# A state-space layer's token sums: four column groups by halves of tokens, and a new order of steps

## The chip, the cores and the metric

The kernel runs on one core of a Trainium2 chip. The metric is device time in microseconds for one execution. The inputs and outputs are float32, and the kernel computes in float32 throughout.

## The reference, cut to what matters

Two layers on 8 batches of 512 tokens with 256 channels. Layer 0 adds an attention (16 heads) and a mixture of 16 experts to the input. Layer 1 adds a state-space block and a linear layer on values rounded to a six-bit grid. The change concerns layer 1 and the weights that it uses:

```python
xz = einsum('bld,ed->ble', xn, in_proj_w); x, z = split(xz, 2)       # 512 channels each
u = silu(conv4(x) + conv1d_b)                                         # causal, four taps, per channel
x_dbl = einsum('bld,rd->blr', u, x_proj_w)                            # 16 dt_low, 16 B, 16 C
delta = softplus(einsum('blr,dr->bld', dt_low, dt_proj_w) + dt_proj_b)
h_t = exp(delta_t * A) * h_(t-1) + delta_t * B_t * u_t                # 512 channels x 16 states
y_t = sum over the 16 states of h_t * C_t  +  u_t * D_param
out = (y * silu(z)) @ out_proj_w.T  +  dequantized(xn) @ dequantized(weight).T + bias
x = x + out
```

## The kernel before, in words

**Layer 0.** `norm_and_route` loads all tokens, normalizes them, chooses experts and scatters the rows to `xs` in DRAM. Then a loop over 32 head groups runs with the experts' matmuls between them. Its order is the program's order on each engine. Before `norm_and_route` the kernel calls `layer1_weights`, which loads all weights of layer 1 through ACT's DMA queue (w_in, w_x, w_dt, w_out, prm, bias, a) and last `wq`, the 256 x 256 weight that is quantized on DVE and POOL (`quantize`) and transposed on PE to `wdT`. The tiles of `wq` and its temporaries lie on the side of SBUF where `xn`, the loaded tokens, comes next.

**Layer 1** has 8 batches. For each there are 16 steps `j`; step `j` treats 32 channels at all 512 tokens. The 128 rows of a step's tiles are four groups of 32 channels, and each group holds four of the 16 states in its free dimension (`SK` = 4, 4 x 512 columns). A step has these parts:

- `decay` (ACT, L715): four exponentials make `da` from the step sizes `step`, which `load_steps` fetches from DRAM for two steps at a time, four times over (one for each group of rows).
- `spread` (PE, L722): a matmul with `sel` copies the 32 rows of `du` (delta times u) onto 128 rows of PSUM.
- `scan` (L728 and L730 on DVE, L734 on POOL): `dbu` = spread times `B`, a scan over 2048 columns gives `h`, and POOL multiplies `h` by `C`. There are four `h` tiles.
- `sums` (PE, L742 and L747), for two steps at once: sums over states. A skip matmul with a diagonal of D_param starts the PSUM tile of a block of 128 channels (every fourth step), then eight matmuls of 512 columns add the two steps' `h` on two groups of 32 columns.
- `gated` (DVE, L751): for a block of 128 channels, y times silu(z).

The loop `for g in range(B * NB)` writes the order by hand: scan(g), then decay and spread of g + 1, then what is due now (`later`: sums two steps after, gated three steps after, and the previous batch's `result` and `put`, four of each, in steps 3 to 7), `load_steps` at even steps, and then one piece of `prepare` for the next batch. `prepare` is a generator of 16 pieces: load x and gather expert rows (two pieces), scale and add and store x (L583 to L585), statistics (L590 to L598), normalize and transpose (L602 to L615), in_proj for x (two pieces, L622 and L626), convolution (two pieces, L635), in_proj for z (two pieces), x_dbl, absolute value to logarithm of the step sizes (L668 to L676), a correction (L678, L680), delta and its store (L685, L686), du and the load of B (L690). The six pieces of `quantize` (L494 to L497; L500; L502 to L506; L509, L510; L512, L513; L515, L516) are called among them. C is loaded after a batch's last step into the one tile that it has. Every engine executes its instructions in this order, and SP issues the loads and stores in this order too.

PSUM holds four banks for `dbu`, one for `spread`, one for `sum` and two (`bank`) for all else. `result` multiplies, for 128 tokens, the quantized rows by `wdT`, the bias by ones, and four blocks of z by `w_out`; ACT copies it to `o`, and `put` adds x on POOL and stores.

A float32 matmul of the program is two matmul instructions in the trace.

Of the kernel before, what the change touches and what calls it, by code (L numbers as in the profile page):

```python
# [34 lines left out]
XR = DTR + 1 + 2 * DS  # L35
# [44 lines left out]
class Kernel:  # L80
# [437 lines left out]
    def layer1_weights(self, w_in, w_x, w_dt, w_out, prm, w_q, bias):  # L518
        nc, one = self.nc, self.weights
        self.w_in = one.tile([P, KC, 2 * DI], F32, name="w_in")  # L520
        nc.scalar.dma_start(out=self.w_in, in_=w_in.rearrange("(kc p) e -> p kc e", p=P))

        self.w_x = one.tile([P, NC, XR], F32, name="w_x")
        nc.gpsimd.memset(self.w_x[:, :, DTR : DTR + 1], 0.0)
        w_x = w_x.rearrange("(c p) r -> p c r", p=P)
        nc.scalar.dma_start(out=self.w_x[:, :, 0:DTR], in_=w_x[:, :, 0:DTR])
        nc.scalar.dma_start(out=self.w_x[:, :, DTR + 1 :], in_=w_x[:, :, DTR:])
        self.w_dt = one.tile([33, DI], F32, name="w_dt")
        nc.scalar.dma_start(out=self.w_dt[0:DTR, :], in_=w_dt)
        nc.scalar.dma_start(out=self.w_dt[DTR : DTR + 1, :], in_=prm[:, DT_B].rearrange("d one -> one d"))  # L530
        self.w_out = one.tile([P, NC, C], F32, name="w_out")
        nc.scalar.dma_start(out=self.w_out, in_=w_out.rearrange("(c p) e -> p c e", p=P))
        self.prm = one.tile([P, NC, 7 + DS], F32, name="prm")
        nc.scalar.dma_start(out=self.prm, in_=prm.rearrange("(c p) k -> p c k", p=P))
        self.bias = self.w_dt[32:33, 0:C]
        nc.scalar.dma_start(out=self.bias, in_=bias)

        self.a = one.tile([P, NB, SK], F32, name="a")
        for q in range(SQ):
            nc.scalar.dma_start(  # L540
                out=self.a[ts(q, 32), :, :],
                in_=prm[:, 7 + SK * q : 7 + SK * (q + 1)].rearrange("(j p) k -> p j k", p=32),
            )
        nc.scalar.activation(self.a, self.a, AF.Exp)
        nc.vector.tensor_single_scalar(self.a, self.a, -1.0, ALU.mult)
# [13 lines left out]

    def in_proj(self, xnT, col):  # L560
        ps = self.bank()
        for kc in range(KC):
            self.nc.tensor.matmul(ps, lhsT=self.w_in[:, kc, ts(col, P)], rhs=xnT[:, kc, :], start=kc == 0, stop=kc == KC - 1)  # L563
        return ps

    def prepare(self, b):
# [17 lines left out]
        nc.gpsimd.tensor_tensor(x, x, y, ALU.add)  # L584
        nc.sync.dma_start(out=rows, in_=x)  # L585
        yield
# [53 lines left out]
        for c in (0, 1):  # L640
            nc.scalar.copy(z[:, c, :], self.in_proj(xnT, NC + c))
        yield
        next(quant, None)
        for c in (2, 3):
            nc.scalar.copy(z[:, c, :], self.in_proj(xnT, NC + c))
# [9 lines left out]
        nc.scalar.activation(x_dbl, ps[:XR, :], AF.Identity, bias=self.ident[:XR, DTR : DTR + 1])  # L655
        me["bc"] = self.dram.tile([2 * DS, N], F32, name="bc")
        nc.sync.dma_start(out=me["bc"], in_=x_dbl[DTR + 1 :, :])
        yield


        def steps_of(c):
            ps = self.bank()
            nc.tensor.matmul(ps, lhsT=self.w_dt[: DTR + 1, ts(c, P)], rhs=x_dbl[: DTR + 1, :], start=True, stop=True)  # L663
            return ps

        s = one.tile([P, NC, N + 3], F32, tag="rows", name="s")[:, :, 3:]
        for c in range(NC):
            nc.scalar.activation(s[:, c, :], steps_of(c), AF.Abs)  # L668
# [5 lines left out]
        me["du"] = [self.six.tile([P, N], F32, name="delta") for _ in range(NC)]  # L674
# [8 lines left out]
        for c in range(NC):  # L683
            delta = me["du"][c]
            nc.vector.scalar_tensor_tensor(delta, steps_of(c), 0.0, delta, ALU.max, ALU.add)  # L685
            nc.sync.dma_start(out=me["steps"][ts(c, P), :], in_=delta)  # L686
# [8 lines left out]
    def load_steps(self, b, c):  # L695

        t = self.three.tile([P, 2, N], F32, name="step")
        rows = self.batch[b]["steps"][ts(c, 64), :].rearrange("(r d) t -> d r t", d=32)
        for q in range(SQ):
            self.nc.sync.dma_start(out=t[ts(q, 32), :, :], in_=rows)  # L700
        self.batch[b]["step", c] = t
# [17 lines left out]
    def spread(self, b, j):  # L719
        c, r = divmod(j, 4)  # L720
        ps = self.spread_pool.tile([P, N], F32, name="spread")
        self.nc.tensor.matmul(ps, lhsT=self.sel[ts(r, 32), :], rhs=self.batch[b]["du"][c][ts(r, 32), :], start=True, stop=True)  # L722
# [13 lines left out]
    def sums(self, b, j):  # L736

        nc, me = self.nc, self.batch[b]
        c, r = divmod(j, 4)
        if r == 0:  # L740
            y = me["sum", c] = self.sum_pool.tile([P, N], F32, name="sum")
            nc.tensor.matmul(y, lhsT=self.skip[:, c, :], rhs=me["u"][:, c, :], start=True, stop=False)  # L742
        y = me["sum", c]
        pair = [(j + i, me.pop(("h", j + i))) for i in range(2)]
        for k in range(SK):
            for i, h in pair:
                nc.tensor.matmul(y[ts(i % 4, 32), :], lhsT=self.sel[:, 0:32], rhs=h[:, k, :], start=False, stop=k == SK - 1)  # L747
# [19 lines left out]
    def result(self, b, j):  # L767
        nc, me = self.nc, self.batch[b]
        ps = self.bank()[:, :C]
        for kc in range(KC):  # L770
            nc.tensor.matmul(ps, lhsT=me["xdT"][:, kc, ts(j, P)], rhs=self.wdT[:, kc, :], start=kc == 0, stop=False)
        nc.tensor.matmul(ps, lhsT=self.ones[32:33, :], rhs=self.bias, start=False, stop=False)
# [132 lines left out]
```

## Time and profile before

| | |
|---|---|
| median of three runs | 2473.65 us (2471.86 to 2474.25) |
| profiled execution | 2472.3 us, span 2470.2 us |
| granted PE clock, mean | 0.87 |
| layer 0, last matmul | ends at 1119.8 us |
| layer 1, first scan | starts at 1216.95 us |
| last of the 128 scans | starts at 2434.95 us |
| one batch, first scan to first scan | 149.6 (batch 0), 156.9 to 157.1 (batches 1 to 6) |

Starts of the 16 scans of a batch, one to the next, batch 3, from step 0: 7.3, 12.0, 7.3, 13.6, 7.1, 13.6, 9.7, 15.2, 7.8, 9.9, 7.3, 9.2, 11.9, 7.8, 7.3, 9.9 us.

How to read it: the page gives busy time of each engine (PE matmuls, PEld weight loads, DVE, ACT, POOL), forty slices of the span with the busy share in tenths, and groups of instructions. A line of the waits says which engine and line waited for which, the total in us, how often, and the longest. A line of the windows gives a stretch, its length, the busy us of each engine with the number of instructions, the granted PE clock and the DMA engines' share. A line of the timeline gives start, duration, engine, line, instruction, out<-in, shapes, count and, in brackets, the idle time before it and what ended it. "128*32 128x512" is a weight tile of 128 rows and 32 columns and an operand of 128 rows and 512 columns.

### The profile page before, as it was taken

Reading aid. Unit: us, or ns where it says so; the run is one execution under the profiler, and the core shown is the slowest. Engines: PE = TensorE matmul, PEld = TensorE weight load, DVE = VectorE, ACT = ScalarE, POOL = GpSimd, SP = SyncE. Lnnn points to the kernel's source line nnn. Section 1 sums busy time; section 2 is a strip of 40 time slices with the busy share of each in tenths; the row PEclk is TensorE's granted clock in tenths of the full one; section 3 lists DMA queues with packets and bytes.
Section 4 is the critical chain, followed back from the end, with each engine's and each line's share of the span. In section 5 each row is a group of like instructions: output and inputs, shape, how many; then the busy total and the mean of one; then the engine's idle time right before and its main releaser. Section 6 shows DMA issues by size and latency. Waiting matters only on the chain.

```text
span 2470.2 us, 21235 instructions
## 1 busy us (share of the span) xinstructions
PE 2022.4 (82%) x8040; PEld 836.1 (34%) x8040; DVE 1546.1 (63%) x1240; ACT 921.0 (37%) x1364; POOL 1006.4 (41%) x513
## 2 busy tenths in 40 slices
PE   2747999999999999995496796987968869688666
PEld 2513444444444444442131231422314224132222
DVE  3423554555555555531498878888788787887784
ACT  0002333333333333432445353353543635436231
POOL 4231010100000000005466668676776767767554
PEclk9958999999999999997687797887968879688778
DMA  6012111121211111101402213032131221402220
GB/s 204 13 49 94 47 61 50 62 81 53 77 46 62 45 62 46 62 6 40 113 17 77 62 51 102 24 88 51 56 90 41 82 57 36 111 31 74 50 60 9
DMA packets 104808, 150.81 MB, mean 61 GB/s; under 512 B 13937, under 2 KB 75122, under 8 KB 102658
## 3 DMA queue, kind: packets, MB, share of 16 engines
q1 hardware_dynamic: 90896, 132.97, 18.3%
q0 software_dynamic: 3072, 8.39, 1.2%
q10 hardware_dynamic: 10738, 8.10, 1.1%
q8 instruction: 63, 1.03, 0.2%
q14 instruction: 39, 0.32, 0.0%
HBM read 113.24 MB, written 36.18 MB: 60 GB/s over the span
## 4 chain that ended last, share of the span: by engine, by line
PE 54%; DVE 19%; POOL 12%; DMA 6%; issue 5%; ACT 4%; SPq 1%; ACTq 0%; DVEq 0%; POOLq 0%
PE s L287 11%; DVE h L730 8%; PE bank L389 7%; POOL h L734 7%; PE bank L379 5%; PE sum L747 5%; PE av L318 5%; DVE dbu L728 4%; PE bank L274 3%; PE bank L563 2%; DMA xs<-xn,to_i 2%; PE spread L722 2%; PE bank L635 2%; PE bank L248 2%; PE bank L663 2%
## 5 line engine op out<-in xcount | busy, mean ns | idle before, releaser
L734 POOL TENSOR_TENSOR h<-h,C 128x2048 f32<-128x2048 f32 x128 | 599.0, 4680 | 372.4 <-DVE h L730 333.2
L730 DVE TENSOR_TENSOR_SCAN h<-da,dbu 128x2048 f32<-128x2048 f32 x128 | 565.8, 4420 | 109.2 <-PE sum L747 77.9
L309 DVE TENSOR_REDUCE qk<-t 128x2 f32<-128x1024 f32 x256 | 313.7, 1225 | 387.5 <-PE t L287 387.5
L305 ACT ACTIVATE e<-s 128x1024 f32<-128x1024 f32 x256 | 262.0, 1024 | 437.5 <-PE t L287 408.3
L715 ACT ACTIVATE da<-step,a 128x511 f32<-128x511 f32 x512 | 325.2, 709 | 251.3 <-DVE h L730 185.3
L722 PE MATMUL spread<-delta,c_sb 32*128 32x512 f32 x256 | 191.3, 835 | 216.2 <-DVE dbu L728 215.8
L728 DVE TENSOR_TENSOR dbu<-spread,B 128x2048 f32<-128x2048 f32 x128 | 293.4, 2292 | 66.9 <-PE spread L722 52.1
L287 PE MATMUL t<-kT,qT 32*128 32x512 f32 x1024 | 298.0, 659 | 8.1 <-DVE qk L309 8.1
L287 PE MATMUL s<-qmT,kT 32*128 32x512 f32 x1024 | 290.4, 643 | 17.1 <-DVE qmT L99 15.6
L747 PE MATMUL sum<-h,c_sb 128*32 128x512 f32 x1024 | 293.1, 725 | 4.9 <-POOL h L734 4.9
L347 POOL TENSOR_TENSOR x<-x,o 128x256 f32<-128x256 f32 x32 | 23.2, 725 | 531.5 <-DVE o L345 531.5
L389 PE MATMUL bank<-w_sb,hT 128*128 128x256 f32 (+1 forms) x768 | 183.6, 382 | 0.0
L261 POOL TENSOR_TENSOR qk<-cos_t,sin_t 128x512 f32<-128x512 f32 x32 | 40.7, 1271 | 316.6 <-DVE sin_t L257 316.4
L379 PE MATMUL bank<-xeT,w_sb 128*128 128x320 f32 x512 | 161.7, 438 | 0.0
L722 PEld LDWEIGHTS spread<-delta,c_sb 32*128 32x128 f32 x256 | 47.9, 231 | 328.7 <-DVE dbu L728 201.2
L747 PEld LDWEIGHTS sum<-h,c_sb 128*32 128x32 f32 x1024 | 63.6, 130 | 249.7 <-issue 238.4
L389 PEld LDWEIGHTS bank<-w_sb,hT 128*128 128x128 f32 (+1 forms) x768 | 126.5, 174 | 43.4 <-issue 16.2
L318 PE MATMUL av<-e,v 128*32 128x512 f32 x1024 | 136.9, 607 | 0.0
L663 PE MATMUL bank<-x_dbl,w_dt 17*128 17x512 f32 x128 | 88.7, 829 | 41.0 <-DVE delta L685 28.1
L563 PE MATMUL bank<-xnT,w_in 128*128 128x512 f32 x256 | 118.1, 606 | 0.0
L287 PEld LDWEIGHTS s<-qmT,kT 32*128 32x128 f32 x1024 | 77.9, 184 | 114.2 <-issue 75.2
L635 PE MATMUL bank<-xs,taps 128*128 128x512 f32 x256 | 113.8, 597 | 1.6 <-ACT xdT L760 1.6
(172 smaller groups left out, 2246.8 us busy)
## 6 DMA issues: line engine op xcount, KB each, us to landing
w_sb<-in_w_dram SPq DMA_DIRECT2D x32, 1024.0 KB, 7.6
step<-steps SPq DMA_DIRECT2D x256, 128.0 KB, 3.1
mid<-x SPq DMA_DIRECT2D x16, 512.0 KB, 3.1
steps<-delta SPq DMA_DIRECT2D x32, 256.0 KB, 2.0
B<-bc SPq DMA_DIRECT2D x32, 256.0 KB, 4.9
C<-bc SPq DMA_DIRECT2D x32, 256.0 KB, 4.9
xs<-zero ACTq DMA_DIRECT2D x1, 5120.0 KB, 27.6
xn<-in_x_dram SPq DMA_DIRECT2D x8, 512.0 KB, 13.3
```

The costliest lines, as they stand in the source:

```text
L287: self.nc.tensor.matmul(ps, lhsT=lhsT[rows, :], rhs=rhs[rows, :], start=True, stop=True)
L305: nc.scalar.activation(e, s, AF.Exp, scale=D**-0.5)
L309: nc.vector.tensor_reduce(self.qk[b % 2][:, m, ds(NG * g + 2 * (1 - pair), 2), D], t, AX.X, ALU.max, negate=True)
L318: self.nc.tensor.matmul(self.av[G][ts(a, 2 * D), :], lhsT=self.v[b % 2][:, m, NG * g + a, :], rhs=self.e[G, m, a // 2][:, a % 2, :], start ...
L379: nc.tensor.matmul(ps[:, :CAP], lhsT=w1_sb[:, kc, ts(f, P)], rhs=xeT[:, kc, :], start=kc == 0, stop=kc == KC - 1)
L389: nc.tensor.matmul(ps[:r, :C], lhsT=hT[:, f, ds(j * P, r)], rhs=w2_sb[:, f, :], start=f == 0, stop=f == NF - 1)
L715: self.nc.scalar.activation(da[:, k, 1:], self.batch[b]["step", c][:, r, 1:], AF.Exp, scale=self.a[:, j, k : k + 1])
L722: self.nc.tensor.matmul(ps, lhsT=self.sel[ts(r, 32), :], rhs=self.batch[b]["du"][c][ts(r, 32), :], start=True, stop=True)
L728: nc.vector.tensor_tensor(dbu, bcast(me.pop(("spread", j))[:, None, :], [P, SK, N]), me["B"], ALU.mult)
L730: nc.vector.tensor_tensor_scan(h.rearrange("p k t -> p (k t)"), self.da[j % len(self.da)].rearrange("p k t -> p (k t)"), dbu.rearrange("p ...
L734: nc.gpsimd.tensor_tensor(h, h, me["C"], ALU.mult)
L747: nc.tensor.matmul(y[ts(i % 4, 32), :], lhsT=self.sel[:, 0:32], rhs=h[:, k, :], start=False, stop=k == SK - 1)
```

## The change

- `sums`: the tile of a block now holds tokens 0 to 255 on rows 0 to 63 and tokens 256 to 511 on rows 64 to 127; the columns are 256 tokens for the block's first 64 channels and 256 for its second. A pair of steps fills four groups of 32 rows with matmuls of 256 columns. The skip matmul becomes four of 64 weight columns and 256 columns.
- z is computed in that layout (`in_proj_z`), and `result` takes it so: for two token blocks at once, on 64 rows each, in both `bank` tiles.
- `spread` takes all 128 rows of a `du` tile with a weight tile (`quarter`) that is zero outside the 32 rows wanted.
- x_proj's output has 96 rows (XR) instead of 49, with dt_low twice, on rows 32 and 64, so that `steps_of` makes two blocks at once on two groups of rows, in both banks.
- The weights of layer 1 other than `wdT` are loaded at the start of layer 1, after the first piece of `prepare(0)`; `w_out` is loaded twice (for two halves of rows), w_dt and dt_low's part of w_x too. Taps and skip are made after three more pieces.
- Buffers: two tiles of step sizes instead of three, five of delta instead of six.
- Order: `result` in steps 3 and 5; its additions one step later and its stores two steps later; `load_steps` ahead of what is due; `quantized_transposed` in step 5; the pieces of `prepare` at steps 12, 13, 14 of the batch before and 0, 1, 2, 4, 6 to 14, with the store of x moved to the next piece.

The diff (cut):

```diff
@@ layer1_weights, now called by layer1 through other_weights
+        self.w_x = one.tile([P, NC, XR], F32, name="w_x")
+        nc.gpsimd.memset(self.w_x, 0.0)
+        for at in (1, 2):
+            nc.scalar.dma_start(out=self.w_x[:, :, ds(32 * at, DTR)], in_=w_x[:, :, 0:DTR])
+        nc.scalar.dma_start(out=self.w_x[:, :, 0:32], in_=w_x[:, :, DTR:])
+        self.w_dt = one.tile([XR, DI], F32, name="w_dt")
+        nc.gpsimd.memset(self.w_dt, 0.0)
+        for at in (32, 64):
+            nc.scalar.dma_start(out=self.w_dt[at : at + DTR, :], in_=w_dt)
+            nc.scalar.dma_start(out=self.w_dt[at + DTR : at + DTR + 1, :], in_=prm[:, DT_B].rearrange("d one -> one d"))
+        for t in range(2):
+            nc.scalar.dma_start(out=self.w_out[ts(t, 64)], in_=w_out.rearrange("(c h p) e -> p c h e", h=2, p=64))
...
+    def in_proj_z(self, xnT, c):
+        ps = self.bank()
+        for h in range(2):
+            for kc in range(KC):
+                for t in range(2):
+                    self.nc.tensor.matmul(
+                        ps[ts(t, 64), ts(h, N // 2)], lhsT=self.w_in[:, kc, ds(DI + c * P + h * 64, 64)],
+                        rhs=xnT[:, kc, ts(t, N // 2)], start=kc == 0, stop=kc == KC - 1,
+                    )
+        return ps
@@ prepare
         nc.gpsimd.tensor_tensor(x, x, y, ALU.add)
+        yield
         nc.sync.dma_start(out=rows, in_=x)
-        yield
...
         def steps_of(c):
-            ps = self.bank()
-            nc.tensor.matmul(ps, lhsT=self.w_dt[: DTR + 1, ts(c, P)], rhs=x_dbl[: DTR + 1, :], start=True, stop=True)
-            return ps
+            both = [self.bank() for _ in range(2)]
+            for i, ps in enumerate(both):
+                rows = ts(1 + i, 32)
+                nc.tensor.matmul(ps, lhsT=self.w_dt[rows, ts(c + i, P)], rhs=x_dbl[rows, :], start=True, stop=True)
+            return both
@@ spread
-        self.nc.tensor.matmul(ps, lhsT=self.sel[ts(r, 32), :], rhs=self.batch[b]["du"][c][ts(r, 32), :], start=True, stop=True)
+        self.nc.tensor.matmul(ps, lhsT=self.quarter[:, r, :], rhs=self.batch[b]["du"][c], start=True, stop=True)
@@ sums
-            nc.tensor.matmul(y, lhsT=self.skip[:, c, :], rhs=me["u"][:, c, :], start=True, stop=False)
+            for g in range(2):
+                for t in range(2):
+                    nc.tensor.matmul(
+                        y[ts(t, 64), ts(g, half)], lhsT=self.skip[:, c, ts(g, 64)], rhs=me["u"][:, c, ts(t, half)],
+                        start=g == 0, stop=False,
+                    )
...
         for k in range(SK):
-            for i, h in pair:
-                nc.tensor.matmul(y[ts(i % 4, 32), :], lhsT=self.sel[:, 0:32], rhs=h[:, k, :], start=False, stop=k == SK - 1)
+            for t in range(2):
+                for i in range(2):
+                    nc.tensor.matmul(
+                        y[ts(2 * t + i, 32), ts(h, half)], lhsT=self.sel[:, 0:32], rhs=pair[i][:, k, ts(t, half)],
+                        start=False, stop=h == 1 and k == SK - 1,
+                    )
@@ result(b, i), for token blocks i and 2 + i
+        both = [self.bank()[:, :C] for _ in range(2)]
+        for t, ps in enumerate(both):
+            for kc in range(KC):
+                nc.tensor.matmul(ps, lhsT=me["xdT"][:, kc, ts(2 * t + i, P)], rhs=self.wdT[:, kc, :], start=kc == 0, stop=False)
+            nc.tensor.matmul(ps, lhsT=self.ones[0:1, :], rhs=self.bias, start=False, stop=False)
         for c in range(NC):
-            nc.tensor.matmul(ps, lhsT=me["z"][:, c, ts(j, P)], rhs=self.w_out[:, c, :], start=False, stop=c == NC - 1)
+            for h in range(2):
+                for t, ps in enumerate(both):
+                    mine = ts(t, 64)
+                    nc.tensor.matmul(
+                        ps, lhsT=me["z"][mine, c, ds(h * N // 2 + i * P, P)], rhs=self.w_out[mine, c, h, :],
+                        start=False, stop=c == NC - 1 and h == 1,
+                    )
@@ layer1
+            first = self.prepare(0)
+            next(first)
+            self.other_weights()
+            for _ in range(3):
+                next(first)
+            self.quarter = self.one.tile([P, 4, P], F32, name="quarter")
+            nc.gpsimd.memset(self.quarter, 0.0)
+            for r in range(4):
+                nc.vector.tensor_copy(self.quarter[ts(r, 32), r, :], self.sel[ts(r, 32), :])
...
-                    for i in range(NT):
-                        at(g + 4 + i, self.result, b, i)
-                        at(g + 5 + i, self.put, b, i, out)
+                    for i in range(2):
+                        at(g + 4 + 2 * i, self.result, b, i)
+                        at(g + 5 + 2 * i, self.added, b, i)
+                        at(g + 6 + 2 * i, self.stored, b, i, out)
+                if j % 2 == 0 and j < NB - 2:
+                    self.load_steps(b, j // 2 + 1)
                 for what, args in later.pop(g, ()):
                     what(*args)
-                if j == 6:
+                if j == 5:
                     self.quantized_transposed(b)
...
-                if j % 2 == 0 and j < NB - 2:
-                    self.load_steps(b, j // 2 + 1)
-                for n, first in ((b + 1, 0), (b + 2, NB - 2)):
-                    if n < B and j >= first:
+                for n, when in ((b + 1, (0, 1, 2, 4, 6, 7, 8, 9, 10, 11, 12, 13, 14)), (b + 2, (12, 13, 14))):
+                    if n < B and j in when:
                         ahead.setdefault(n, self.prepare(n))
                         next(ahead[n], None)
```

## The prediction

> **What bounds the kernel now.** I read the page first, then the waits of the six full batches of layer 1 (1366 to 2308 us), the windows of one batch, and its timeline. Lines of the page:
>
> ```profile
> span 2470.2 us, 21235 instructions
> PE 2022.4 (82%) x8040; PEld 836.1 (34%) x8040; DVE 1546.1 (63%) x1240; ACT 921.0 (37%) x1364; POOL 1006.4 (41%) x513
> DVE  3423554555555555531498878888788787887784
> PE 54%; DVE 19%; POOL 12%; DMA 6%; issue 5%; ACT 4%; SPq 1%; ACTq 0%; DVEq 0%; POOLq 0%
> ```
>
> The shares hide two stages. Up to slice 18 attention and experts run, PE at 9 tenths; the change leaves that loop alone. From 1217 us the 128 scans run, with DVE at 8 tenths and PE not far behind. The windows of one batch (157 us, scan 2 of it to scan 2 of the next):
>
> ```profile
> core 0: us, PE busy (x) PEld busy (x) DVE busy (x) ACT busy (x) POOL busy (x), PEclk, DMA share, GB/s
> 1542.20:1559.30 17.10, 14.48 (x28) 7.14 (x28) 16.93 (x8) 6.07 (x11) 11.21 (x8) 0.50 0.02 4
> 1559.30:1631.00 71.70, 69.78 (x209) 27.63 (x209) 54.69 (x19) 34.69 (x52) 44.84 (x16) 1.00 0.13 39
> 1631.00:1699.00 68.00, 43.92 (x93) 10.24 (x91) 55.95 (x31) 29.24 (x44) 52.79 (x21) 0.70 0.40 103
> ```
>
> DVE has 127.6 us of work, so 29 us of a batch are its waits. In the middle stretch PE is full at a granted clock of 1.00 and DVE has gaps; before and after it PE runs at 0.50 and 0.70. The waits name the gaps:
>
> ```profile
> DVE h L730 <- PE sum L747: 52.7, 30, 3.1
> DVE dbu L728 <- PE spread L722: 51.6, 18, 6.1
> DVE stats L590 <- POOL x L584: 21.9, 6, 4.1
> DVE h L730 <- ACT da L715: 18.5, 6, 3.1
> DVE delta L685 <- PE bank L663: 15.9, 12, 1.6
> ```
>
> The three on PE are 120.2 us, 20.0 a batch; the other two 6.7. That is all a batch can gain: 27 us.
>
> **Part 1, the sums.** Two places of the timeline, for one weighing (layer 0) and one pair of sums, each with the instruction that follows:
>
> ```profile
> 1044.94 1.06 PE L318 MATMUL av<-e,v 128*32 128x512 f32 x8
> 1045.94 0.33 PE L274 MATMUL bank<-c_sb,qk 128*128 128x128 f32 x1
> ...
> 1618.19 3.63 PE L747 MATMUL sum<-h,c_sb 128*32 128x512 f32 x16
> 1621.75 0.63 PE L653 MATMUL bank<-u,w_x 128*49 128x512 f32 x1
> ```
>
> A float32 matmul is two instructions; one of 512 columns takes 0.43 us alone (in_proj: 8 in 3.63). Eight on four column groups took 1.00, four at a time; sixteen on two groups took 3.56, two at a time. After the change a pair is 32 instructions of 256 columns (0.215 each; L389's eight took 1.73) on four groups: 8 x 0.215 = 1.72 us, against 3.44. A batch has eight pairs: 13.8 us of PE at full clock, twice that at half. Bounds: 1.72, and 3.44 if twice the instructions cannot be fed at that rate. I take 1.72, since layer 0 shows the same four groups with four different operands.
> The Trainium skill ("TensorE: Matmul & The Clock Gate", section "Wait — 56ns, not 53.3ns?") says that with decoding in firmware each matmul costs about 62 ns at least; by that a pair would be 2.0 us, an estimate; the busiest microsecond of this trace started 21 loads and matmuls together, which does not decide it.
>
> **Part 2, the new layout.** z by halves: 16 instructions of 256 columns a channel block, two at a time on 64 columns, 1.72 us as before. Skip: eight in pairs, 0.86, as before. Result: for two token blocks 8 + 4 + 32 instructions, the 32 in pairs on 64 rows, 28 x 0.215 = 6.0 us, as two results before (14 x 0.215 each). No row shows 64-wide pairs; the nearest are the 32-wide groups above, so I take "in pairs"; the other end (one at a time) is the second rival. Spread over 128 rows keeps its 0.86; the 0.19 lost at each change of shape (1.05 from spread to the next) goes on one side: worth 0 to 3 us of PE a batch, taken as 0. Step sizes in pairs on two row groups: 8 matmuls at 0.86 become 4 x 0.86, 3.4 us of PE; but a pair holds both banks, so PE then waits for ACT or DVE, with the next spread queued behind it on PE and dbu behind that.
>
> **Part 3, the order.** I replay a batch at full clock from the rows: dbu 2.30 plus scan 4.42 and gaps, 6.9 a step; L734 4.5. Scan-to-scan times, before and after:
> - 2 to 3: 7.3 -> 11.7. L494, L495, L497 (1.2, 3.6, 0.35) move here; L495 ends with POOL's L734, as now.
> - 3 to 4: 13.9 -> 10.1. Scan 4 needs h of group 0, so sums(0): spread 1.05, result pair 6.0 + 0.4, skip 1.05, sums 1.72. Now half of the way is at half clock.
> - 4 to 5: 7.1 -> 6.9. 5 to 6: 13.6 -> 9.1 (1.05 + 6.4 + 1.75).
> - 6 to 7: 9.7 -> 13.1. L502, L505, L506 (0.7, 4.9, 1.1) come here; L505 again ends with L734.
> - 7 to 8: 15.2 -> 6.8. Two conv blocks (6.9 each) queue now with results before spread and sums; afterwards each has a step.
> - 8 to 9: 7.8 -> 7.3. 9 to 10: 9.9 -> 12.4: POOL has L509 to L513 (4 x 2.35) and two L734 in steps 7 and 8, 18.4 us in two steps that now take DVE 14.1; L515 waits 4.4.
> - 10 to 11: 7.3 -> 7.5. 11 to 12: 9.4 -> 6.8 and 12 to 13: 11.9 -> 9.3 (L678 one step later).
> - 13 to 14: 7.9 -> 13.6. Four L685 (2.75), and their matmuls now stand behind sums(10): 4.4 of waits at half clock.
> - 14 to 15: 7.3 -> 7.4. 15 to 0: 9.9 -> 10.4 (sums(12) behind a spread that waits for L690).
> - 0 to 1: 7.1 -> 8.5, 1 to 2: 12.1 -> 7.9. L584 moves ahead of the C loads, so L590 (1.7) waits no more. The next wait is still there: SP issues C behind the last L734, then the step sizes; from that L734's end (1680.9) to da (1691.7) were 10.8 us. With L690 (4.9) and L584 (2.4) now both in step 14, that L734 ends 13.3 after scan 15 starts instead of 10.4; da(2) ends 13.4 later, 26.7, against 29.3 to scan 2 now.
> Sum: 157.0 -> 148.8.
>
> On SP the stores of the output go behind the step loads and one step after their addition, so the hold of 13.03 us (two of them, at 1581) no longer stands in front of loads; with two buffers for step sizes the older is free two steps before, so the third was cover of nothing. Five delta buffers: the third waits for spread(11), done by then: 0.
>
> **The clock takes part back.** Rows: spread's two instructions take 1.12 at full clock and 2.07 at half; after gaps the clock was 0.50 for 17.1 us here. With less work PE has more gaps. If step 3 starts at half, result and sums end 5.6 us later (19 of 28 slots at 0.43). I cannot tell from the trace, take half of it, 2.8: 151.6, a gain of 5.4. Bounds: 148.8 and, all lost, 157.
> The Trainium skill (same page, section "What's actually happening") puts the drop after one idle window of 3.4 us; by it the 2.8 us gap that my replay has before step 3 would drop nothing, and the batch would be 148.8. The trace speaks against taking that whole: the clock fell at 1631.0 after 6.8 us in which PE was busy for 5.0.
>
> **Part 4, weights moved.** Kernel start: wq is issued at 12.52 behind eleven other loads, its POOL work starts at 16.80 and the x load at 27.64 waits for all that. Now wq goes second; POOL is busy with fills until 11.6, so -5.2 (bounds 0 and -11.3). Layer 1's start: taps and skip (11.6 us of POOL, from 1118.57) move behind the gathers, good for up to -10; but sixteen loads are issued on ACT in front of the scaling of y. Twelve took 11.3 us at the start, 0.94 each; w_x waits for a fill on POOL behind two gathers (about 1123), fifteen more end at 1137, the last lands 3.0 later, exp 0.3, scaling 2.1: 1142.5 against 1138.2. I take +4 (bounds -10, +14).
>
> **The sum.** Six batches 6 x 5.4 = -32.4; batch 0 (149.6, without results) -3; batch 7 (126.4: four waits of about 1.4 for half-clock sums go, its two double results cost 1.1 and 1.5) -3; start -5.2; layer 1's start +4. Together -39.6. The profiled execution took 2472.3 (span 2470.2 and 2.1 around it), the median is 1.35 above: 2472.3 - 39.6 + 1.35 = 2434.
>
> **Rivals.** (a) The clock holds, and L505 and L515 wait less: 146 a batch, 11 x 6, another 11 in batches 0 and 7, start terms -1.2: 2395. For it: 71.7 us at 1.00 now. Against: PE was full then. (b) Slower: 64-wide matmuls run one at a time. Result +3.4 in 3 to 4 and in 5 to 6, skip +0.9, z +3.4 in two steps of which some 2 shows: +10 a batch, 161.6, +4.6 x 8, start terms -1.2: 2509. It decides once more than half of the pairs fail (5.4 of 10). Against it: 32-wide groups run together. (c) Half clock in steps 3, 7 and 13 and POOL's moved work eat all 8.2; start terms alone: 2472. (d) The change does not do what it says: sums stay at 3.44, +1.7 in 3 to 4 and 5 to 6 and 3.4 in 15 to 0: 158.4, 2484.
>
> **How the numbers follow.** Forecast 0.50, (a) 0.18, (b) 0.11, (c) 0.14, (d) 0.07. The forecast's own range is 2404 to 2464 (4 us a batch each way); to hold 8 in 10 it reaches to 2380 for most of (a) and to 2492 for (c) and (d). About 0.2% is what can be told from no change: forecast nearly all faster, (c) split with a third within, (b) and (d) slower: 0.72, 0.06, 0.22.
>
> **What would show it.** L747: 32 instructions of 256 columns in 1.7 us at full clock; "h <- PE sum" down from 8.8 a batch to under 4; "dbu <- spread" from 8.6 to under 2; new waits of L515 on L513 (about 4) and of L685 on L663 (about 4); 7 to 8 near 7 us, 3 to 4 near 10 to 13; x load near 22.4; first scan near 1216. A batch of 157 with PE's clock under 0.75 means (c); starts of 64-wide matmuls 0.2 apart instead of in twos, (b).

## The result, and the profile after

The changed kernel takes 2487.99 us (median of 2483.63, 2485.43, 2490.56, 2491.57); the kernel before took 2473.14 beside it. The ratio is 1.0059, 95% interval 1.0040 to 1.0079. So it is slower by 0.6%, where 1.6% faster was forecast. The profiled execution took 2483.63 us. The lines of its page:

```profile
span 2481.9 us, 25001 instructions
PE 1858.3 (75%) x9896; PEld 866.0 (35%) x9896; DVE 1586.1 (64%) x1244; ACT 917.3 (37%) x1364; POOL 990.6 (40%) x516
DVE  4423455555555455431498798787888888888784
PE 50%; DVE 22%; POOL 11%; issue 8%; DMA 5%; ACT 3%; SPq 0%; ACTq 0%; DVEq 0%; POOLq 0%
```

PE lost 164 us of work, as it should. But DVE, on which the scans run, has 40 us more with practically the same instructions (1244 against 1240). That second number is where the account starts: an engine's work can only grow like this if the same instructions take longer.

The sums do what the change says. The timeline of one pair, with the instructions that follow:

```profile
1616.76 1.93 PE L785 MATMUL sum<-h,c_sb 128*32 128x256 f32 x32
1618.62 1.73 PE L584 MATMUL bank<-xnT,w_in 128*64 128x256 f32 x14
```

32 instructions of 256 columns in 1.86 us, where the old pair took 3.56. The 64-wide pairs run together too: the result's 32 (L820) take 3.72 us for two token blocks.

The windows of one batch (scan 2 to scan 2 of the next), and the waits of DVE in the six full batches; columns as before:

```profile
1545.00:1552.00 7.00, 3.92 (x10) 2.34 (x11) 6.88 (x5) 3.81 (x9) 6.66 (x7) 0.51 0.00 0
1552.00:1647.60 95.60, 77.07 (x429) 37.20 (x427) 80.63 (x27) 46.44 (x69) 61.97 (x22) 0.93 0.15 45
1647.60:1701.70 54.10, 23.57 (x122) 7.88 (x122) 46.72 (x26) 19.34 (x33) 38.95 (x20) 0.62 0.42 107
```

```profile
DVE h L760 <- PE sum L785: 74.1, 19, 9.0
DVE dbu L758 <- PE spread L752: 23.7, 16, 3.3
DVE delta L715 <- PE bank L690: 16.9, 16, 2.1
DVE xd L515 <- POOL temps L513: 11.7, 6, 2.2
DVE more L706 <- ACT more L701: 3.8, 6, 0.6
```

This batch still takes 156.7 us (the six full batches 158.5 on average) and DVE is busy for 134.2 of it (127.6 before). Its waits fell from 29 to 22 us: the change did win 7 us of waits, and DVE's own instructions took them back.

**Where they took it.** Single instructions of DVE and POOL, first the changed kernel's step 12, then the kernel before at the same instruction:

```profile
1642.91 4.42 DVE L760 TENSOR_TENSOR_SCAN h<-da,dbu 128x2048 f32<-128x2048 f32 x1
1647.41 4.52 POOL L764 TENSOR_TENSOR h<-h,C 128x2048 f32<-128x2048 f32 x1 [2.37 <-DVE h L760]
1647.96 6.12 DVE L706 SCALAR_TENSOR_TENSOR more<-more,s 128x2048 f32<-128x2048 f32 x1 [0.63 <-ACT more L701]
```

```profile
1638.39 2.27 DVE L678 SCALAR_TENSOR_TENSOR more<-more,s 128x2048 f32<-128x2048 f32 x1
1638.62 6.45 POOL L734 TENSOR_TENSOR h<-h,C 128x2048 f32<-128x2048 f32 x1 [2.86 <-DVE h L730]
```

It is the same instruction on the same shapes. In the kernel before it starts 0.23 us ahead of POOL's multiplication by C and takes 2.27 us, and POOL takes 6.45: it ends 4.41 us after DVE has ended, about its usual whole time. In the changed kernel it waits 0.63 us for ACT, POOL starts first with its usual 4.52 us and ends at 1651.93, and DVE ends 2.15 us after that. So whichever starts first runs alone; the other makes next to no headway until it ends. I call this the hold. POOL can bear it, as it idles 2.4 us in a step; DVE cannot.

Over the seven batches that have one prepared beside their scans, three instructions are newly held: L706 from 2.47 to 6.10 us (mean), L515 from 1.82 to 5.52, L502 from 0.69 to 4.64, 79 us in all. Two are mostly free of it: L505 from 4.89 to 1.04 and L495 from 3.58 to 1.42 (still held in two batches of seven), 42 us. The difference, 37 us, is nearly all of the page's 40; of the rest, 1.6 us were added ahead of the first scan.

The Trainium skill ("SBUF — State Buffer", section "SBUF: two separate sides") describes an SBUF port pair that VectorE and GpSimd share as a lock: the one that starts first has it for the whole instruction and the other blocks. The rows above agree, 6.45 us for POOL and 6.12 for DVE in the two orders.

### The profile page after: what moved, and what is told of

It is laid out like the page before. It is cut to its first block, busy times and chain, and to the rows that moved or that the text cites. A ratio compares the mean times of both kernels' runs of the same rounds, so it can differ in the third digit from the quotient of the medians.

```text
span 2481.9 us, 25001 instructions
## 1 busy us (share of the span) xinstructions
PE 1858.3 (75%) x9896; PEld 866.0 (35%) x9896; DVE 1586.1 (64%) x1244; ACT 917.3 (37%) x1364; POOL 990.6 (40%) x516
## 4 chain that ended last, share of the span: by engine, by line
PE 50%; DVE 22%; POOL 11%; issue 8%; DMA 5%; ACT 3%; SPq 0%; ACTq 0%; DVEq 0%; POOLq 0%
PE s L287 11%; DVE h L760 10%; PE bank L389 6%; DVE dbu L758 6%; PE bank L379 5%; PE av L318 5%; POOL h L764 4%; PE sum L785 3%; PE bank L274 3%; DMA xs<-xn,to_i 2%; PE spread L752 2%; PE bank L820 2%; PE bank L248 2%; PE bank L690 2%; PE bank L814 1%
## 5 line engine op out<-in xcount | busy, mean ns | idle before, releaser
L764 POOL TENSOR_TENSOR h<-h,C 128x2048 f32<-128x2048 f32 x128 | 578.8, 4524 | 382.8 <-DVE h L760 332.7
L760 DVE TENSOR_TENSOR_SCAN h<-da,dbu 128x2048 f32<-128x2048 f32 x128 | 565.8, 4421 | 108.2 <-PE sum L785 82.9
L752 PE MATMUL spread<-delta,quarter 128*128 128x512 f32 x256 | 203.3, 887 | 390.4 <-DVE dbu L758 331.1
L752 PEld LDWEIGHTS spread<-delta,quarter 128*128 128x128 f32 x256 | 52.5, 252 | 479.5 <-DVE dbu L758 357.9
L785 PE MATMUL sum<-h,c_sb 128*32 128x256 f32 x2048 | 156.0, 456 | 6.7 <-POOL h L764 6.7
L379 PEld LDWEIGHTS bank<-xeT,w_sb 128*128 128x128 f32 x512 | 91.4, 193 | 52.2 <-issue 25.9
L785 PEld LDWEIGHTS sum<-h,c_sb 128*32 128x32 f32 x2048 | 69.7, 130 | 111.4 <-issue 64.1
L274 PEld LDWEIGHTS bank<-c_sb,qk 128*128 128x128 f32 x384 | 46.1, 143 | 151.4 <-issue 119.4
```

The source lines that it names most:

```text
L379: nc.tensor.matmul(ps[:, :CAP], lhsT=w1_sb[:, kc, ts(f, P)], rhs=xeT[:, kc, :], start=kc == 0, stop=kc == KC - 1)
L752: self.nc.tensor.matmul(ps, lhsT=self.quarter[:, r, :], rhs=self.batch[b]["du"][c], start=True, stop=True)
L760: nc.vector.tensor_tensor_scan(h.rearrange("p k t -> p (k t)"), self.da[j % len(self.da)].rearrange("p k t -> p (k t)"), dbu.rearrange("p ...
L764: nc.gpsimd.tensor_tensor(h, h, me["C"], ALU.mult)
L785: nc.tensor.matmul(y[ts(2 * t + i, 32), ts(h, half)], lhsT=self.sel[:, 0:32], rhs=pair[i][:, k, ts(t, half)], start=False, stop=h == 1 and ...
```

## The experiments

Theories: **the hold** as above; **the clock**, TensorE at half clock delivering sums and spread late; **the layout**, halves and 64-wide matmuls that cost what they give; and later **the queue**, work in front of the sums in TensorE's order. All ratios are to the kernel before. Names with `ready` have the moves of ready_first. The last column goes by the changed kernel's lines: in the kernel before L706 is L678, and in split_quant the four are L705, L514, L501 and L504.

| kernel | median us | ratio, 95% interval | DVE busy us | L706 / L515 / L502 / L505, mean us |
|---|---|---|---|---|
| kernel before | 2473.14 | 1 | 1546.1 | 2.47 / 1.82 / 0.69 / 4.89 |
| changed kernel | 2487.99 | 1.0059 (1.0040 to 1.0079) | 1586.1 | 6.10 / 5.52 / 4.64 / 1.04 |
| dbu_first | 2419.89 | 0.9775 (0.9735 to 0.9816) | 1546.4 | 4.10 / 5.52 / 2.25 / 1.05 |
| no_mult | 2342.56 | 0.9457 (0.9418 to 0.9496) | 1486.8 | 2.29 / 1.20 / 0.68 / 0.69 |
| ready_first | 2406.59 | 0.9717 (0.9678 to 0.9757) | 1528.3 | 2.27 / 1.89 / 4.37 / 1.29 |
| old_order | 2454.79 | 0.9905 (0.9875 to 0.9935) | 1582.1 | 4.52 / 4.91 / 4.39 / 1.29 |
| sums_first | 2425.32 | 0.9803 (0.9775 to 0.9831) | 1586.6 | 6.11 / 5.52 / 4.67 / 1.04 |
| ready_sums | 2370.58 | 0.9575 (0.9549 to 0.9600) | 1524.8 | 2.27 / 1.48 / 0.67 / 4.89 |
| ready_sums3 | 2391.18 | 0.9656 (0.9630 to 0.9682) | 1524.8 | 2.27 / 1.49 / 0.67 / 4.89 |
| before_ready | 2495.39 | 1.0067 (1.0031 to 1.0103) | 1542.1 | 2.27 / 1.20 / 4.38 / 1.64 |
| split_quant | 2365.38 | 0.9547 (0.9507 to 0.9588) | 1493.7 | 2.27 / 1.32 / 0.67 / 0.67 |
| one_later | 2457.58 | 0.9918 (0.9892 to 0.9944) | 1572.9 | 5.04 / 5.19 / 4.64 / 1.04 |
| one_later_z | 2448.93 | 0.9869 (0.9814 to 0.9924) | 1560.7 | 6.65 / 1.20 / 0.67 / 4.88 |
| before_dbu | 2461.12 | 0.9941 (0.9921 to 0.9961) | 1534.5 | 4.58 / 3.37 / 1.93 / 1.04 |

Beside these stand four with filler matmuls, told below.

### no_mult: without POOL's multiplication

```diff
-        nc.gpsimd.tensor_tensor(h, h, me["C"], ALU.mult)
```

> The changed kernel without GpSimd's multiplication by C (the sums take the states without it; that part of the computation is left out). Theory 'the hold': with no 4.5 us of GpSimd behind each scan, L706, L515 and L502 take their own 2.4, 1.2 and 0.7 us; VectorE is busy some 90 us less (1586 to about 1495), and the sums need not wait for the product, so that the scan's 72.8 us of waits for them fall too: 2350 to 2400 us. Rival 'the clock': these three stay at 4.6 to 6.1 us, as something else makes them slow; only the waits fall: 2420 to 2470 us.

Groups of DVE's instructions from 1210 us on (count, busy us, mean ns, idle before):

```profile
L706 DVE SCALAR_TENSOR_TENSOR more<-more,s 128x2048 f32<-128x2048 f32 x7 | 16.0, 2286 | 0.7
L515 DVE TENSOR_TENSOR xd<-xd,temps 128x1024 f32<-128x1024 f32 x7 | 8.4, 1201 | 0.0
L502 DVE TENSOR_SCALAR temps<-temps 128x1024 int32<-128x1024 int32 x7 | 4.8, 682 | 0.0
```

2342.56 us, 7 below the range. The three fall to their own durations once POOL's instruction is gone; nothing else on DVE was touched, and its work falls by 99 us. That shows the hold. One part of the expectation missed: the scan's waits for the sums did not fall (90.0 us from 1210 us on, 82.9 in the changed kernel), so the multiplication was not what made the sums late.

### dbu_first: the unaffected instruction ahead of the held ones

```diff
                     self.spread(*after)
+                    self.inputs(*after)     # dbu, taken out of scan; scan keeps the scan and POOL's product
```

> The changed kernel with one order changed on VectorE: dbu of the next step (it reads PSUM) stands right behind the scan, and what layer 1 prepares on VectorE (and the product with z) stands behind that. Theory 'the hold': a VectorE instruction on SBUF alone that begins after GpSimd's multiplication by C has begun does nothing until that multiplication ends. In the changed kernel the instruction behind the scan is held so at L706 (6.1 us, 2.45 before), L515 (5.5) and L502 (4.6). With the 2.3 us of dbu ahead of them they should take about 2.3 us less each: some 3.8, 3.2 and 2.4 us, 6.9 us a batch, about 48 us in all at most: 2440 us (2435 to 2465, where other waits take the place). Rival 'the clock': the batches are long since TensorE at half clock delivers the sums late (72.8 us of waits of the scan); then the order on VectorE gives nothing, 2480 to 2492 us.

```profile
L515 DVE TENSOR_TENSOR xd<-xd,temps 128x1024 f32<-128x1024 f32 x7 | 38.7, 5523 | 16.8 <-POOL temps L513 16.8
L706 DVE SCALAR_TENSOR_TENSOR more<-more,s 128x2048 f32<-128x2048 f32 x7 | 28.7, 4099 | 1.2 <-ACT more L701 1.1
L502 DVE TENSOR_SCALAR temps<-temps 128x1024 int32<-128x1024 int32 x7 | 15.7, 2247 | 0.0
```

2419.89 us. L706 and L502 lose 2.0 and 2.4 us as expected. dbu, with one operand in PSUM, keeps its 2.30 us beside POOL's product (2.29 before). L515 stays at 5.52: it waits for L513, and POOL goes from L513 straight into the next product, so the same race is run later. The time is below the expected range: the gain of 68 us is more than the 40 us off DVE, and other waits went with it (for one, see the chain further down).

### ready_first: ready before the scan ends

```diff
-        next(quant, None)                   # L515: in the second z part, behind L513 of the part before
+        next(quant, None)                   # now in the x_dbl part, a step later
-                for n, when in ((b + 1, (0, 1, 2, 4, 6, 7, 8, 9, 10, 11, 12, 13, 14)), ...
+                for n, when in ((b + 1, (0, 1, 2, 4, 5, 6, 7, 8, 9, 10, 12, 13, 14)), ...
+                # gated (the product with z) is called behind the part of prepare
```

> The changed kernel with the three held instructions made ready before the scan ends, so that VectorE goes on with them without a gap: L515 one step behind GpSimd's L513, the step sizes' part one step earlier (conv, z, x_dbl and steps each a step earlier, L706 stays at step 12), the product with z behind the prepared part. Theory 'the hold': whichever engine begins first goes on, the other waits. So L706, L515 and L502 at 2.4, 1.2 and 0.7 us, 12 us a batch less on VectorE, 75 us in all; GpSimd's multiplication behind them grows from 4.5 to 5 to 7 us; since the conv now lies beside result(1), part of it is lost to waits for TensorE: 2410 to 2450 us. Rival 'the clock': no gain, 2480 to 2500 us.

2406.59 us, just below the range. L706 takes 2.27 and L515 1.89 us, and POOL's product grows from 4.52 to 4.69 on average: the hold now falls on the engine that can bear it. L502 stayed at 4.4: it waits 0.9 us for POOL's L500, and POOL goes on from there into its next product, 0.08 us ahead of L502.

### old_order and before_ready: layout and order crossed

old_order has the changed kernel's layout with the steps in the order before. before_ready is the kernel before with the changed kernel's order and ready_first's moves; only its results stay one token block each, in steps 3 to 6, and its transposes in step 6.

> The changed kernel's layout, weights' loading and step sizes in pairs, with the order of steps of the kernel before (one part of layer 1's preparation at each step, two of the batch after next at steps 14 and 15, load of steps behind, transposes at step 6). Theory 'the hold': the order is what costs; the held instructions are then those of before (VectorE busy near 1546 us, not 1586) and TensorE's shorter sums are a gain: 2430 to 2460 us. Rival 'the layout': halves and 64-wide matmuls cost as much as they give, 2475 to 2495 us in either order.

> The kernel before (sums on 64 columns of 3.44 us for 32 matmuls, weights loaded as before, step sizes one by one) in ready_first's order. Theory 'hold and order apart from the layout': the held instructions are gone here too, VectorE busy 1510 to 1525 us instead of 1546; TensorE has 137 us more to do than with the new layout and now waits show it: 2420 to 2450 us, so the layout is worth 15 to 45 us under an order without holds. Rival 'the layout gives nothing': 2400 to 2412 us, as ready_first.

old_order took 2454.79 us, as the hold theory said in time, but not in its reason: DVE is at 1582 us, so the old order on the new layout has as much held time as the new order. Which instructions are held differs from kernel to kernel in the table; neither order alone settles it. The layout, with the weights and step sizes that came with it, gains 18 us in the old order. before_ready took 2495.39, outside both expectations, and DVE was at 1542 us there, since L502 (4.38) and L495 (3.65) were held. Under this order the old layout is 89 us slower than the new one; the scan's waits for the sums are 117 us there, 61 in ready_first. So what the layout is worth depends on the order: 18 us in the old one, 89 in this.

### one_later and one_later_z: one instruction

```diff
-        next(quant, None)                   # L515, ahead of the second z part
+        next(quant, None)                   # L515, in the x_dbl part (one_later: this alone)
+                # one_later_z: gated is called behind the part of prepare as well
```

> The changed kernel with one instruction moved: L515 (and GpSimd's L516 behind it) a step later, so that it no longer waits for GpSimd's L513 and is ready when scan 10 ends. Theory 'the hold': L515 5.5 us and 1.7 us of wait become 1.2 to 1.9 us and none, up to 5.5 us a batch, 38 us in all: 2445 to 2465 us. If the sums or TensorE set that step anyway (14.0 us, TensorE busy for 7.7 of it): 2470 to 2488 us.

> one_later (2457.6 us, L515 still 5.2 us there) with the product with z behind the prepared part, which it stood ahead of at steps 6 and 10. The hold in its finer form (only the instruction directly behind the scan goes ahead of GpSimd's multiplication): L515 now follows the scan and takes 1.2 to 1.9 us, 3.5 us a batch less, while L502 (0.7) only hands its hold to L505 (4.9): 2425 to 2440 us. If it was not the product with z that let the multiplication in, L515 stays above 5 us: 2450 to 2462 us.

In one_later L515 is ready when scan 10 ends, and still took 5.19 us. The product with z (L792) stands ahead of it there; it reads PSUM, takes 0.67 us beside POOL, and meanwhile POOL's product (L764) starts:

```profile
1620.29 0.67 DVE L792 TENSOR_TENSOR z<-sum,z 128x512 f32<-128x512 f32 x1
1620.45 4.52 POOL L764 TENSOR_TENSOR h<-h,C 128x2048 f32<-128x2048 f32 x1 [1.00 <-DVE h L760]
1620.87 5.19 DVE L515 TENSOR_TENSOR xd<-xd,temps 128x1024 f32<-128x1024 f32 x1
```

The time of one_later lies in the hold's range all the same, but not for its reason: L515's wait for L513 went (14.6 us in the changed kernel) and L706 took 5.04 us instead of 6.10. With L792 behind L515, DVE and POOL in the timeline of one_later_z:

```profile
1582.31 0.67 DVE L502 TENSOR_SCALAR temps<-temps 128x1024 int32<-128x1024 int32 x1
1582.47 4.87 POOL L764 TENSOR_TENSOR h<-h,C 128x2048 f32<-128x2048 f32 x1 [6.24 <-DVE h L760]
1583.01 4.88 DVE L505 TENSOR_SCALAR y<-temps 128x1024 f32<-128x1024 f32 x1
...
1619.91 1.20 DVE L515 TENSOR_TENSOR xd<-xd,temps 128x1024 f32<-128x1024 f32 x1
1620.08 5.43 POOL L764 TENSOR_TENSOR h<-h,C 128x2048 f32<-128x2048 f32 x1 [0.54 <-DVE h L760]
1621.03 0.69 DVE L792 TENSOR_TENSOR z<-sum,z 128x512 f32<-128x512 f32 x1
```

L515 takes 1.20 us. And the first three lines give the finer form: going first protects one instruction only. L502 goes ahead of POOL, whose product starts 0.16 us later; L505, directly behind L502, pays. The time is above the expected range, as L706 rose to 6.65 us and the waits for the sums to 96.4. The two kernels can't be told apart well: 2433.9 to 2460.2 us against 2450.2 to 2462.0.

### sums_first, ready_sums, ready_sums3, split_quant: what stands in front

```diff
-                for what, args in later.pop(g, ()):
+                for what, args in sorted(later.pop(g, ()), key=lambda e: e[0] == self.result):
```

sums_first has this line alone, on the changed kernel; ready_sums has it with ready_first's edits. ready_sums3 gives ready_sums the steps (0, 1, 2, 3, 5, 6, 7, 8, 9, 10, 12, 13, 14). split_quant is ready_sums with L500 in the first part of `quantize` and L502, L505 and L506 one to a step.

> The changed kernel with the sums issued ahead of the result at steps 3 and 5 (in the changed kernel the result's 3.7 us stand ahead of them on TensorE, and scans 4 and 6 wait for the h buffers that the sums free). Theory 'queue order': the scan's 72.8 us of waits for the sums are mostly the result ahead of them: 3 to 5 us a batch less, 2455 to 2475 us, and the holds (L706 6.1, L515 5.5, L502 4.6 us) stay. Rival 'TensorE full': TensorE is busy through all of steps 3 and 5, so the wait only moves to what stands behind, 2480 to 2492 us.

> ready_first (2406.6 us) with the sums ahead of the result as well. 'Queue order': its 5.1 us of wait at scan 4 in each batch goes, and part of the 14.1 us at step 5: 2375 to 2395 us. Rival 'TensorE full' (11.9 of 11.9 us busy at step 3 there, 8.7 of 8.7 at step 6): 2400 to 2410 us.

> ready_sums with the parts of steps 4 and 5 at steps 3 and 5, so that GpSimd's product L500 lies two steps ahead of L502. Theory 'the hold': L502, held for 5.0 us in ready_first since it waited 0.9 us for L500, takes 0.7 us: 4 us a batch, 25 us in all, 2350 to 2385 us. Against it: two in_proj groups now stand with the result and the sums at step 3 on TensorE; if TensorE is full there, 2375 to 2410 us.

> ready_sums (2370.6 us) with the quantization's three VectorE instructions on its temporaries (L502, L505, L506) one to a step in place of all three behind one scan, and GpSimd's L500 two steps ahead of L502. In ready_sums L502 went first (0.67 us) and L505 behind it took 4.9 us. Theory 'the hold', in its finer form: only the instruction that directly follows the scan goes ahead of GpSimd's multiplication; the next one finds that multiplication running. So each of the three should take 0.7 us: 4.2 us a batch, 29 us in all, 2340 to 2352 us. Rival 'other limits': step 5 (13.0 us) is then set by ScalarE's decays or by the sums: 2355 to 2371 us.

sums_first took 2425.32 us with DVE's work unchanged at 1586.6: the scan's waits for the sums in layer 1 fell by 65 us, from 82.9 to 17.5, and the time by 63; more than the 13 to 33 us expected: the 3 to 5 us a batch were too low for 12 us of waits, and batch 7 alone, left out there, fell from 124.6 to 109.4. So the result in front of the sums is a second, separate loss. It is in the kernel before too, but smaller: scan 4 waits about 2 us for the sums in each of the six full batches there and scan 6 not at all, where the changed kernel, with two results at once ahead of the sums, has 4.9 to 9.0 and 3.1 to 4.8. The two edits add in the main: ready_sums took 2370.58 us, 117 below the changed kernel where the two alone gave 81 and 63, and 103 below the kernel before, in four executions within 0.4 us. ready_sums3 is 21 us slower than ready_sums, and L502 at 0.67 us was so in both: its reason fell away, and the parts moved to steps 3 and 5 made the spread late (waits of dbu for it 58.8 us against 39.1). In split_quant all three of `quantize` take 0.67 us, 31 us less work for DVE, yet the time falls by 5. Waits of DVE from 1210 us on (its lines are one lower than in the other kernels):

```profile
DVE dbu L757 <- PE spread L751: 67.0, 28, 7.7
DVE h L759 <- ACT da L744: 27.0, 15, 2.9
```

The wait for the spread rose from 39.1 to 67.0, 7.7 us of it in step 7 of each full batch: TensorE is busy for all of steps 3 to 8 but 0.7 us (batch 3), and DVE arrives earlier only to wait. So the rival 'other limits' had the time right, though it named other waits. That is the limit of this line of edits. split_quant, at 0.9547 (0.9507 to 0.9588), is the best kernel found.

### The filler: fill_after, fill_ready, fill1_after, fill1_split

```diff
+        for _ in range(n + 1 if (j - 1) % NB in steps else 1):
             self.nc.tensor.matmul(ps, lhsT=self.quarter[:, r, :], ...)
```

n is 8 in the first two and 1 in the others.

> The changed kernel with the spread matmul repeated eight more times (same values) at steps 0 to 2, 6 and 11 to 15, where TensorE idles most, to keep its clock from falling to half. Rival 'the clock' (the prediction's 2.8 us a batch for half clock, and its case c): the granted clock rises from 0.859 to 0.90 or more and the time falls by 10 to 40 us, 2450 to 2478 us. Theory 'the hold': the clock is not what ends the waits at those steps; within 0.4%, 2480 to 2500 us.

> ready_sums with the same filler at steps 0 to 2 and 10 to 15. Once the holds are gone VectorE waits for the spread (39 us), bank L690 (22 us) and the sums (20 us), all TensorE's work at half clock in steps 12 to 2. 'The clock': 2340 to 2365 us. 'Not the clock': the filler only lengthens TensorE's queue, 2370 to 2390 us.

> fill_after again with one repeat of the spread in place of eight (each repeat took 0.86 us at full clock, so that eight were 6.9 us a step and made dbu wait). Rival 'the clock': the granted clock rises above 0.859 and the 2.8 us a batch that the prediction put on half clock come back, 2465 to 2482 us. 'The hold': no gain, 2484 to 2505 us.

> split_quant (2365.4 us) with one repeat of the spread at steps 0 to 2 and 10 to 15. With the holds gone VectorE waits there for TensorE's work at half clock (bank L690 21.8 us, sums 23 us). 'The clock': 2340 to 2362 us. 'Not the clock': 2366 to 2385 us.

2664.90, 2576.93, 2523.66 and 2380.27 us, all slower than without filler; only the last lies in a stated range, that of 'not the clock'. The first two were mis-sized: a repeat is two instructions of 0.43 us, so eight are 6.9 us a step, and dbu waits for the last of them; the granted clock rose to 0.934 and 0.955 at that price. With one repeat it was 0.861 (0.859 without) and 0.892 (0.872 without). So these fillers raised the clock only by standing in the way of the work, and no kernel gained from it. This doesn't measure what half clock costs; that stays open, and with it the 2.8 us a batch that the prediction set aside.

### before_dbu: the hold in the kernel before

> The kernel before with dbu of the next step right behind the scan, as in dbu_first. The hold is in the kernel before too (L505 4.9 us, L495 3.6 us, where 1.0 and 0.2 are their own): each 2.3 us less, 4.6 us a batch, 2435 to 2455 us. 'TensorE sets it': its sums are longer there (3.44 us a step's pair), the scan's 77.9 us of waits for them grow by as much, 2465 to 2476 us.

2461.12 us, a gain of 12, below the expected one and between the two ranges. The edit is dbu_first's. L505 fell from 4.89 to 1.04 and L495 from 3.58 to 1.18 us, but L678 rose from 2.47 to 4.58, L515 from 1.82 to 3.37 and L502 from 0.69 to 1.93: with dbu in front POOL goes first (its product by C never takes more than 4.56 us, where it took up to 6.53 before), and the instructions that had won their race now lose it by the shorter rest. The kernel before already paid a hold, on other lines.

## Why the prediction was wrong

Forecast for the profiled execution: 2472.3 - 39.6 = 2432.7 us. It took 2483.6, which is 51 more. The same terms, measured: the six full batches 158.5 us on average against 151.6, +41; batch 0 151.7 against 146.6, +5; batch 7 124.6 against 123.4, +1; first scan at 1218.3 against 1215.7, +2.6; after the last scan +1. In the six full batches, from first scan to first scan, DVE's work rose by 36 us (769.7 to 805.9) and its waits fell by 27; the forecast took the work as unchanged and the waits 32 lower. So of the 41 us 36 are work that grew and 5 are waits.

- **Part 1** held: 1.86 us against 1.72 taken. Rivals (b) and (d), the slow 64-wide matmuls and the sums that stay at 3.44, are refuted by the rows above, and (d)'s 2484 is near the result for a reason that isn't its own. The 2.0 us that would follow from the 62 ns of the Trainium skill ("TensorE: Matmul & The Clock Gate", section "Wait — 56ns, not 53.3ns?") for decoding in firmware did not show: 32 instructions in 1.86 us are 58 ns each.
- **Part 4** held at the kernel's start: the x load is issued at 22.48 us against 22.4. The first scan came 2.6 us later than the two start terms gave; no run tried where that lies.
- **Part 3 failed**, the replay of the order. Its steps against batch 2 of the trace: 12 to 13 9.3, measured 13.5; 8 to 9 7.3 and 10.1; 9 to 10 12.4 and 14.0; 3 to 4 10.1 and 11.7; the other way 2 to 3 11.7 and 9.8. The largest miss, 4.2 us a batch, is "L678 one step later", put down as a mere shift. I had seen that L495 "ends with POOL's L734" and that L505 "again ends with L734", but took this as fixed to those two instructions and not as a race that each instruction runs anew. L678 had won its race by 0.23 us and lost it after the move by 0.55; L515, which I gave only a wait of 4.4, waited 1.7 to 2.2 us and was then held. Net of the two that I had kept held and that came mostly free, this is 37 us more work for DVE (79 - 42), beside the 51 us by which the time was missed; no run undoes these holds alone.
- **The chain behind it** goes with the step from 8 to 9. L502 was held for 4.65 us in step 6, so dbu and then the spread came late; PE had been idle for 5.56 us, and its next work (PE, then DVE in the last line) starts at half clock (granted 0.50 from 1599.5 to 1602.9 us, 0.95 in the next 3.4 us):

```profile
1599.57 1.98 PE L776 MATMUL sum<-u,skip 128*64 128x256 f32 x8
1601.47 2.77 PE L785 MATMUL sum<-h,c_sb 128*32 128x256 f32 x32
1604.17 7.14 PE L659 MATMUL bank<-xs,taps 128*128 128x512 f32 x16
1611.15 1.02 PE L752 MATMUL spread<-delta,quarter 128*128 128x512 f32 x2
1612.21 2.30 DVE L758 TENSOR_TENSOR dbu<-spread,B 128x2048 f32<-128x2048 f32 x1 [3.22 <-PE spread L752]
```

  Skip took 1.98 us there (1.08 in step 3), sums 2.77 (1.93), so the convolution ended late and dbu waited 3.22 us for the spread behind it. dbu_first, with L502 at 2.25 and with dbu and so the spread issued earlier, has that step at 7.0 us. This link is read from the two traces; no run changed the clock alone.
- **Waits**: the scan's wait for the sums was to fall under 4 us a batch; it is 12.4 (74.1 / 6). The replay had the result ahead of the sums in steps 3 and 5, so the place was right, and its own 10.1 and 9.1 us already leave 5.4 us of waits there, more than that sign. Measured, scans 4 and 6 wait 9.7 us a batch. sums_first shows that this queue was a loss of its own, which the forecast took as given. In batch 3, where L495 lost its race, the result started at half clock (granted 0.57 and then 0.50 from 1715.4 to 1722 us) and scan 4 waited 9.0 us: 164.0 us for that batch. Races that fall differently from batch to batch may be behind the spread of the four executions (8 us); only one of them was profiled. The wait of dbu for the spread is 4.0 us a batch against under 2. L715's wait for L690 is 2.8 a batch against 4 forecast.
- **Rival (a)** asked for a clock that holds; its mean fell from 0.87 to 0.859. **Rival (c)**, half clock and POOL's moved work eating the gain, was nearest in what it blamed: POOL did take the gain, but through the hold, which (c) did not name. Its sign, a batch of 157 with PE's clock under 0.75, is met by half: batch 2 takes 156.7 at 0.80 (0.81 before).

## What to carry to other kernels

Before moving a VectorE instruction, look in the trace at which side of GpSimd's long instruction it starts: being ready a few tenths of a microsecond earlier or later made 2.3 or 6.1 us of the same instruction. Put the one SBUF instruction of VectorE that matters directly behind the work that releases GpSimd, ready beforehand, and no short PSUM instruction ahead of it; spread several of them one to a step. When busy time of an engine rises without new instructions, compare mean durations line by line before looking for waits.

## What the runs showed of the hardware that was not expected

The hold is decided per instruction: with L502 running first (0.67 us) POOL still got in ahead of L505, which directly followed it (4.89 us). Instructions with an operand in PSUM were not held: the scan stayed at 4.36 to 4.42 us, dbu at 2.27 to 2.30 and the product with z at 0.63 to 0.69 in all kernels, whatever POOL did. Not every instruction on SBUF alone is held either: with POOL's product running, in the changed kernel, the reduction L494 took 1.21 us (1.19 alone), the statistics L614 0.40 to 0.43 (0.40 to 0.41) and the reciprocal L497 0.35 (0.35). Held were, on float32 or int32 in SBUF, TENSOR_SCALAR (L495, L502, L505) and the two kinds with two tensors as operands (L515, L706).
